# Single-head attention and ternary ffn in one loop, with the reads of the mixture's sums spread over it

## The chip, the core and the metric

The kernel runs on one core of a Trainium2 chip. Its engines work side by side, each through its own queue in order: PE (TensorE; its weight loads are shown as PEld), DVE (VectorE), ACT (ScalarE), POOL (GpSimd) and SP (SyncE, which here only issues DMAs). They wait for one another through semaphores. The metric is the device time of one execution in microseconds (us); lower is better.

## The reference, cut to what matters

A decoder of four layers works on x of 128 sequences x 64 positions x 128 features, with a context of the same shape. Each layer has an attention, a cross attention and an ffn; after each step comes `x = layernorm(x + step(x))`. The change touches the three steps of layer 0:

```python
# step 1, "attn": a mixture of 8 experts, two of them for each token
probs = softmax(x @ gate_w + gate_b); topw, topi = top_k(probs, 2); topw /= topw.sum()
out_e = gelu_tanh(x @ w1[e] + b1[e]) @ w2[e] + b2[e]
y = sum over the two chosen e of topw * out_e
# step 2, "xattn": one head of width 128
q, k, v = x @ Wq + bq, ctx @ Wk + bk, ctx @ Wv + bv
y = softmax(q @ k.T / sqrt(128)) @ v
# step 3, "ffn": ternary weights
W = clip(round(W / scale), -1, 1), scale = max(mean(|W|), 1e-8)     # for W1 and W2
y = gelu(x @ W1.T + b1) @ W2.T + b2
```

Everything is fp32.

## The kernel before, in words

The 8192 tokens stay in SBUF as 16 chunks `X[0..15]` of 512 tokens (four tiles of 128 tokens x 128 features). The twelve steps run one after the other (`steps`, L1890); each runs over the chunks. A tile framework gives out buffers, sets the semaphores, and places the instructions of each engine in a fixed order by its own estimate of when each could run; inside the mixture's loop the order is written out (`issue_after`).

**The mixture** (`Sorted`, L472; driven by `moe_top2`, L912). The tokens of a batch are sorted by expert into groups of 256 rows. Batches are chunks 0 to 4 and 5 to 15. `all_groups` (L848) runs over the groups of both batches: SP loads the expert's weights (L730), POOL gathers the rows from DRAM by indirect DMA (L747), PE transposes them (L758), hidden layer (L772, L774) and output (L785, L786) follow, and SP writes the rows to a DRAM buffer `l_rout` (L787). Beside it run generators (`aside`): the plan of the next batch, and `finish` (L794) of the batch before. `finish` takes a step for each token tile: two indirect reads on POOL (L805), and three steps later on DVE the weighted sum (L815, L817) and statistics (L818); when a chunk's four tiles are summed, `end` (L820) makes its LayerNorm on DVE (L827 to L357, a reciprocal square root in several small instructions) and ACT applies it (L378). A cost list and a length (`total - 4` groups) say when each generator takes its next step. The first batch's sums lie in the loop of the second batch's groups. The second batch's sums are a generator of its own, `moe_end` (L897).

**The single-head attention** (`xattn_single`, L949) is a software pipeline over turns i = -3 to 15 with five steps a turn (L1036): `scores` of chunk i+1 (L999, then maximum, Exp and sum), `turned_weights` of i (transposes, L1014), `projections` of i+2 (q, k by `projected`, L937; v with its bias as a matmul of bf16 rows that `bv` holds, L981), `values` of i (L1026, L1032, LayerNorm applied on ACT) and `sources` of i+3. `sources` calls `moe_done` (L917): it steps `moe_end` four times, and further until the chunk is summed; then it transposes the context (L930) and x (L325).

**The ternary ffn** (`ffn_ternary`, L1042) first makes the ternary weights on ACT, DVE and PE (L1049 to L1063), then goes through the chunks with `hidden` of c ahead of `output` of c-1 (`pipelined`, L406). `hidden` transposes x (L325), adds the output bias to x on POOL (`with_bias`, L393) and makes four hidden blocks with Gelu (L1072, L1074). `output` (L1082) makes 16 products of 128 x 128, each matmul instruction recorded twice; DVE adds x (L399) and takes the statistics (L366, L368), and POOL applies the LayerNorm (`ln_apply`, L380).

The differential attention `attn_diff` follows. It uses two buffers `VX` (L1095), which POOL fills with zeros and two columns of a mask (L1114, L1116) before use.

PSUM has eight banks: `bank` (L315) takes from three of them, `wide` (L318) from five.

Of the kernel before, what the change touches and what calls it, by code (L numbers as in the profile page):

```python
# [22 lines left out]
P = 128  # L23
# [211 lines left out]
def tile_decoder(ctx: ExitStack, tc: tile.TileContext, a, out):  # L235
# [69 lines left out]
    def row(n):  # L305
        return rows[:, _ROW_AT[n][0] : _ROW_AT[n][1]]
# [64 lines left out]

    def ln_apply(c, r, mv, y, store=False, on_act=False):
        if on_act:
            s = sm.tile([P, TPC], F32, tag="lns", name="lns")
            V.scalar_tensor_tensor(s, mv[:, :, 0], -1.0, y, ALU.mult, ALU.mult)
        for t in range(TPC):
            if on_act:
                A.activation(X[c][:, t, :], r[:, t, :], AF.Identity, bias=s[:, t : t + 1], scale=y[:, t : t + 1])  # L378
            else:
                G.tensor_scalar(X[c][:, t, :], r[:, t, :], mv[:, t, 0:1], y[:, t : t + 1], ALU.subtract, ALU.mult)  # L380
        if store:
            nc.sync.dma_start(out=out_v[c], in_=X[c])

    def layernorm(c, r, store=False, on_act=False):

        v = sm.tile([P, TPC], F32, tag="lnv", name="lnv")
        mv = ln_stats(r, v)
        ln_apply(c, r, mv, rsqrt(v, TPC, "ln"), store, on_act)

# [82 lines left out]
    class Sorted:  # L472
# [4 lines left out]
        def __init__(s, which, top, batches, src, wg, bias, act, cap=None, store=False, scattered=None):  # L477
            s.which, s.top, s.batches, s.src, s.wg, s.bias, s.act, s.cap, s.store = which, top, batches, src, wg, bias, act, cap, store
            s.at, s.loaded, s.done, s.carry = {}, {}, set(), None
            s.row_tiles, s.turned, s.between = {}, {}, None  # L480
# [367 lines left out]
        def all_groups(s):  # L848
# [10 lines left out]
            for b in range(nb):  # L859
# [5 lines left out]
                if b > 0:  # L865
                    aside.append([s.finish(b - 1), [1] * s.finish_steps(b - 1), 0, 2, total - 4])
                for g in range(total):
# [23 lines left out]
                for x in aside:  # L891
                    assert x[2] == len(x[1]) and next(x[0], None) is None
            s.output(*last)


    moe = Sorted("l0", 2, MOE_BATCHES, [a["x"]], "gatew", "gateb", AF.Gelu_apprx_tanh)
    moe_end = moe.finish(len(MOE_BATCHES) - 1)  # L897

# [18 lines left out]
    def moe_done(c):  # L917

        for _ in range(TPC):
            next(moe_end, None)  # L920
        while c not in moe.done:
            next(moe_end)
# [25 lines left out]

    def xattn_single():  # L949
# [3 lines left out]
        st = {}  # L953

        rest = work("tmp", (P, D), "bvrest")
        V.tensor_copy(rest, row("l0xbv"))
        bv = work("tab", (P, 2, P), "bvparts", BF16)
        part = work("tmp", (P, D), "bvpart", BF16)
        V.memset(bv[:, 0, :], 1.0)
        for k in range(3):  # L960
            V.tensor_copy(part, rest)
            if k == 0:
                V.tensor_scalar(bv[:, 1, :], part, ident[:, 0:1], None, ALU.mult)
            else:
                V.scalar_tensor_tensor(bv[:, 1, :], part, ident[:, k : k + 1], bv[:, 1, :], ALU.mult, ALU.add)
            if k < 2:
                V.tensor_tensor(rest, rest, part, ALU.subtract)
        ring = work("e", (P, 4, TPC, D), "v1")
# [6 lines left out]
        def projections(c):  # L975
            s = st[c]
            s["q"] = projected(w[:, 0, :], s["xT"], "qT", col("l0xbq"))
            s["k"] = projected(w[:, 1, :], CTX[c], "kT", col("l0xbk"))

            v = bank("v1_ps")  # L980
            mm(v.rearrange("p (n d) -> p n d", n=4), bv[:32, 0, :], bv[:32, 1, None, :].to_broadcast([32, 4, D]), start=True, stop=False, skip_group_check=True)  # L981
            for f in range(2):
# [52 lines left out]

        for i in range(-3, NC):  # L1036
            for step, c in ((scores, i + 1), (turned_weights, i), (projections, i + 2), (values, i), (sources, i + 3)):
                if 0 <= c < NC:
                    step(c)


    def ffn_ternary():  # L1042
        w = W[2]
        wt = work("tab", (P, 2, FK, P), "tern")
        for n in range(2):
            src = w[:, 4 * n : 4 * n + 4, :].rearrange("p k m -> p (k m)")
            t = work("tmp", (P, 512), "absw")
# [39 lines left out]

# [6 lines left out]
    V.tensor_copy(identh, ident)  # L1094
    VX = [const.tile([P, BPC * 8 * 34], F32, tag=f"vx{n}", name=f"vx{n}") for n in range(2)]  # L1095

# [786 lines left out]
    def ffn_switch():  # L1883
# [32 lines left out]
```

## Time and profile before

| | us |
|---|---|
| runs shown: median (lowest to highest) | 3282.17 (3279.47 to 3289.09) |
| the profiled execution, its own time | 3278.03 |
| its span, first to last instruction | 3276.3 |
| mean granted TensorE clock | 0.946 |

Busy time over the span, and of the groups that the change touches:

| row | count | busy us | mean ns | idle before, and what ended it |
|---|---|---|---|---|
| PE, whole span | 47184 | 2882.3 (88%) | | |
| DVE, whole span | 7074 | 1973.2 (60%) | | |
| ACT, whole span | 3106 | 1614.1 (49%) | | |
| POOL, whole span | 1548 | 1521.4 (46%) | | |
| L805 POOL indirect read got<-l_rout | 192 | 194.4 | 1012 | 148.7, most by issue |
| L747 POOL indirect gather aux<-x | 156 | 159.9 | 1025 | 56.9, most by issue |
| L380 POOL x<-xb (all steps) | 304 | 238.6 | 797 | 267.5, by DVE ln_y L345 |
| L772 PE h_ps<-ebT,rw (both mixtures) | 992 | 241.2 | 387 | 8.6, most by DMA rw |

The counts of L805 and L380 include later steps; of L805, 40 lie between 207.5 and 347.8 us (first batch) and 88 between 411.9 and 526.7 us (second batch).

How to read the rows of the profile: a group's row gives line, engine, operation, the tile written and the tiles read with their shape, the count, busy time and mean. A row of waits says which engine and line waited for which engine and line: us in total, times, the longest. A row of the timeline gives start, duration and instruction, "x4" for four merged ones, and in brackets how long the engine idled before and what ended that. A row of stages gives for each engine the busy time in that window and, in brackets, the number of instructions. Matmuls overlap, so the cost of one is read from the distance between starts.

### The profile page before, as it was taken

What the parts mean: (1) busy time and instruction counts of PE and PEld (TensorE: products, weight loads), DVE (VectorE), ACT (ScalarE), POOL (GpSimd) and SP (SyncE); (2) the same over time, 40 slices, a digit from 0 to 9 for tenths busy, and PEclk for the clock granted to TensorE, in tenths of its full rate; (3) what the DMA queues carried; (4) which work ended last, traced back from release to release, by engine and by line L of the source; (5) the groups of instructions that cost most, each with busy time, mean ns of one, the idle gap of its engine ahead of it and who ended that gap; (6) DMA issues with size and microseconds to landing.
All of it is one profiled execution on the core that took longest, in us unless ns stands there. A gap on an engine that the chain in (4) does not pass through costs nothing. (4 is left out here: it accounts for less than half of the span.)

```text
span 3276.3 us, 110323 instructions
## 1 busy us (share of the span) xinstructions
PE 2882.3 (88%) x47184; PEld 2115.1 (65%) x47184; DVE 1973.2 (60%) x7074; ACT 1614.1 (49%) x3106; POOL 1521.4 (46%) x1548
## 2 busy tenths in 40 slices
PE   5999967999987999999999989998888569998993
PEld 3888834666665777766677767774444336776793
DVE  3733267557777666433256656666778886666246
ACT  3544457445543565333355545643444555654553
POOL 4477473454555344311234445556566322446154
PEclk9999988999998999999999989989988789998997
DMA  5578710000002000000000000000000000001684
GB/s 142 160 214 248 220 52 28 8 1 3 3 3 76 19 4 4 6 1 1 5 11 4 4 5 4 4 13 1 1 1 2 9 1 16 18 15 46 181 266 147
DMA packets 142459, 159.23 MB, mean 49 GB/s; under 512 B 16720, under 2 KB 118096, under 8 KB 141968
## 3 DMA queue, kind: packets, MB, share of 16 engines
q1 hardware_dynamic: 128064, 123.65, 12.7%
q0 software_dynamic: 13184, 27.03, 3.2%
q8 instruction: 370, 6.06, 0.7%
q10 hardware_dynamic: 720, 1.50, 0.1%
q14 instruction: 121, 0.99, 0.1%
HBM read 121.44 MB, written 30.67 MB: 46 GB/s over the span
## 5 line engine op out<-in xcount | busy, mean ns | idle before, releaser
L1183 DVE TENSOR_REDUCE m<-s_ps 128x8 f32<-128x512 f32 x640 | 397.5, 683 | 144.4 <-PE s_ps L1411 50.8
L1232 ACT ACTIVATE e<-t_ps 128x512 f32<-128x512 f32 x640 | 330.0, 601 | 150.7 <-PE t_ps L1225 150.2
L380 POOL TENSOR_SCALAR x<-xb,lnmv,ln_y 128x128 f32<-128x128 f32 x304 | 238.6, 797 | 267.5 <-DVE ln_y L345 267.5
L1250 PE MATMUL av_ps<-vx,e 128*64 128x18 f32 (+1 forms) x10240 | 341.3, 216 | 5.6 <-issue 5.3
L1250 PEld LDWEIGHTS av_ps<-vx,e 128*64 128x64 f32 x10240 | 322.9, 140 | 25.9 <-issue 18.7
L1127 POOL TENSOR_SCALAR eb<-qT,small 128x512 f32<-128x512 f32 x80 | 131.2, 1640 | 431.5 <-ACT qT L943 200.9
L774 ACT ACTIVATE hT<-h_ps,aux 128x256 f32<-128x256 f32 x496 | 206.6, 470 | 208.4 <-PE h_ps L772 102.3
L1213 PE MATMUL t_ps<-eb,kT 32*64 32x128 f32 x10240 | 281.3, 285 | 4.4 <-DVE m L1183 2.2
L805 POOL DMA_INDIRECT got<-l_rout,pli x192 | 194.4, 1012 | 148.7 <-issue 57.7
L772 PE MATMUL h_ps<-ebT,rw 128*128 128x256 f32 x992 | 241.2, 387 | 8.6 <-DMA rw<-in_l0w_dram 4.5
L785 PEld LDWEIGHTS yg<-rw,hT 128*128 128x128 f32 x1984 | 241.8, 192 | 6.4
L1213 PEld LDWEIGHTS t_ps<-eb,kT 32*64 32x64 f32 x10240 | 198.1, 132 | 71.1 <-DVE m L1183 25.6
L785 PE MATMUL yg<-rw,hT 128*128 128x128 f32 x1984 | 242.1, 276 | 0.0
L1175 PE MATMUL s_ps<-eb,qT 32*64 32x256 f32 x5120 | 217.5, 399 | 20.8 <-POOL eb L1127 9.8
L786 DVE TENSOR_TENSOR yo<-yg,aux 128x256 f32<-128x256 f32 x124 | 52.6, 424 | 267.5 <-PE yg L785 264.4
L1255 DVE RECIPROCAL rc<-av_ps 128x32 f32<-128x32 f32 (+1 forms) x192 | 61.7, 321 | 240.7 <-PE av_ps L1250 240.3
L772 PEld LDWEIGHTS h_ps<-ebT,rw 128*128 128x128 f32 x992 | 182.8, 194 | 31.1 <-DVE ebT L760 6.3
L747 POOL DMA_INDIRECT aux<-in_x_dram,plt x156 | 159.9, 1025 | 56.9 <-issue 26.8
L1125 ACT ACTIVATE eb<-qT,small 128x512 f32<-128x512 f32 x160 | 106.8, 715 | 129.3 <-POOL qT L1352 124.1
L380 POOL TENSOR_SCALAR x<-r,lnmv,ln_y 128x128 f32<-128x128 f32 x68 | 54.4, 813 | 225.0 <-DVE ln_y L345 225.0
L1127 POOL TENSOR_SCALAR eb<-kT,small 128x512 f32<-128x512 f32 x80 | 145.9, 1823 | 22.1 <-ACT kT L945 11.3
L1175 PEld LDWEIGHTS s_ps<-eb,qT 32*64 32x64 f32 x5120 | 114.3, 134 | 60.2 <-issue 15.2
(429 smaller groups left out, 6414.5 us busy)
## 6 DMA issues: line engine op xcount, KB each, us to landing
rw<-in_l0w_dram SPq DMA_DIRECT2D x78, 512.0 KB
rw<-in_l3w_dram SPq DMA_DIRECT2D x46, 512.0 KB
l_rout<-yo SPq DMA_DIRECT2D x124, 128.0 KB
aux<-xd SPq DMA_DIRECT2D x46, 128.0 KB
aux<-in_l0b_dram SPq DMA_DIRECT2D x78, 66.0 KB
xd<-vx SPq DMA_DIRECT2D x5, 1024.0 KB
x<-in_x_dram SPq DMA_DIRECT2D x16, 256.0 KB
cin<-in_ctx_dram SPq DMA_DIRECT2D x16, 256.0 KB
```

The lines of the kernel that those rows point to most:

```text
L380: G.tensor_scalar(X[c][:, t, :], r[:, t, :], mv[:, t, 0:1], y[:, t : t + 1], ALU.subtract, ALU.mult)
L747: s.gather = G.indirect_dma_start(out=eb[:, i, :], out_offset=None, in_=x[:, :], in_offset=bass.IndirectOffsetOnAxis(ap=tokens[:, 2 * g + ...
L772: s.pe = mm(ps[:, j * GR : (j + 1) * GR], w1[:, (k + j) * P : (k + j + 1) * P], ebT, start=True, stop=True)
L774: s.act_ins = A.activation(hT[k + j], ps[:, j * GR : (j + 1) * GR], s.act, bias=v[:, k + j : k + j + 1])
L785: s.pe = mm(y[:, i * P : (i + 1) * P], hT[k][:, i * P : (i + 1) * P], w2[:, k, :], start=(k == 0), stop=(k == FK - 1))
L805: s.gather = G.indirect_dma_start(out=got[i][k][:, t, :], out_offset=None, in_=s.rout[b][:, :], in_offset=bass.IndirectOffsetOnAxis(ap=whe ...
L1127: ins = (G if h == 2 else V).tensor_scalar(dst, x, mine, None, ALU.mult)
L1175: mm(ps[g][j * S : (j + 1) * S, u * 256 : (u + 1) * 256].rearrange("p (h k) -> p h k", h=4), rows32(s["q"], g)[:, b], rows32(s["eb"], g)[: ...
L1183: last = V.tensor_reduce(s["m"][:, g, 2 * hf : 2 * hf + 2, :].rearrange("p t h -> p (t h)"), ps[g].rearrange("p (n k) -> p n k", k=S), AX. ...
L1213: mm(ps[g][i * S : (i + 1) * S].rearrange("p (a u j q) -> p a u j q", u=2, a=2, j=2)[:, :, u, j, :], rows32(s["k"], g)[:, b], rows32(s["eb ...
L1232: last = A.activation(e[:, g, :], ps[g], AF.Exp, scale=scale)
L1250: mm(av[j * S : (j + 1) * S, 8 * (u - u0) + n, :], ev[:, n // 2, n % 2, u, j, :], vx[:, 2 * (2 * hf + u) + j, n, :], start=True, stop=True,)
```

## The change

- Attention and ffn run in one loop of turns i = -3 to 17. The ffn is two chunks behind: in turn i `turned`, `hidden` and `output` work on chunk i-2, `hidden` and `output` of a chunk in the same turn. The ternary weights are made after turns -3 and -2.
- `summed`, a single step of the mixture's sums, stands in four places of a turn. `moe_done` only steps further while the chunk isn't summed.
- The first batch's sums get twice the length (`stretch = 2`), so that some half of their steps are left when the group loop ends; `moe_sums` takes those first and then the second batch's.
- The ffn's output bias is no longer added to x on POOL; it opens the output's accumulation as a matmul of bf16 rows (`bias_rows`), as the attention's value bias did. Both sets of rows, and the hidden blocks, lie in the `VX` buffers, which are defined earlier.
- `ln_apply` can run on DVE; the ffn does so for chunks 0 to 7 and stays on POOL for 8 to 15.
- q and k of the attention take their PSUM from `wide` and no longer from `bank`.

```diff
@@ ln_apply
-                G.tensor_scalar(X[c][:, t, :], r[:, t, :], mv[:, t, 0:1], y[:, t : t + 1], ALU.subtract, ALU.mult)
+                (V if on_dve else G).tensor_scalar(X[c][:, t, :], r[:, t, :], mv[:, t, 0:1], y[:, t : t + 1], ALU.subtract, ALU.mult)
@@ Sorted.all_groups
-                    aside.append([s.finish(b - 1), [1] * s.finish_steps(b - 1), 0, 2, total - 4])
+                    s.rest = s.finish(b - 1)
+                    aside.append([s.rest, [1] * s.finish_steps(b - 1), 0, 2, s.stretch * (total - 4)])
@@
-    moe_end = moe.finish(len(MOE_BATCHES) - 1)
+    moe.stretch = 2
+
+    def moe_sums():
+        yield from moe.rest
+        yield from moe.finish(len(MOE_BATCHES) - 1)
+
+    moe_end = moe_sums()
@@ moe_done
-        for _ in range(TPC):
-            next(moe_end, None)
         while c not in moe.done:
             next(moe_end)
@@
-    def projected(w, srcT, name, bias=None):
+    def projected(w, srcT, name, bias=None, bank=bank):
...
+    VX = [const.tile([P, BPC * 8 * 34], F32, tag=f"vx{n}", name=f"vx{n}") for n in range(2)]
+
+    def bias_rows(bias, place, name):
+
+        both = VX[place][:, 2048:2176].bitcast(BF16).rearrange("p (z d) -> p z d", z=2)
+        rest, part = work("tmp", (P, D), f"{name}rest"), work("tmp", (P, D), f"{name}part", BF16)
+        V.tensor_copy(rest, bias)
+        V.memset(both[:, 0, :], 1.0)
+        for k in range(3):
+            V.tensor_copy(part, rest)
+            if k == 0:
+                V.tensor_scalar(both[:, 1, :], part, ident[:, 0:1], None, ALU.mult)
+            else:
+                V.scalar_tensor_tensor(both[:, 1, :], part, ident[:, k : k + 1], both[:, 1, :], ALU.mult, ALU.add)
+            if k < 2:
+                V.tensor_tensor(rest, rest, part, ALU.subtract)
+        return both[:32, 0, :], both[:32, 1, None, :].to_broadcast([32, 4, D])
@@ xattn_single, projections
-            s["q"] = projected(w[:, 0, :], s["xT"], "qT", col("l0xbq"))
-            s["k"] = projected(w[:, 1, :], CTX[c], "kT", col("l0xbk"))
+            s["q"] = projected(w[:, 0, :], s["xT"], "qT", col("l0xbq"), wide)
+            s["k"] = projected(w[:, 1, :], CTX[c], "kT", col("l0xbk"), wide)
@@
-        for i in range(-3, NC):
-            for step, c in ((scores, i + 1), (turned_weights, i), (projections, i + 2), (values, i), (sources, i + 3)):
-                if 0 <= c < NC:
-                    step(c)
-
-
-    def ffn_ternary():
-        w = W[2]
+        b2 = bias_rows(row("l0fb2"), 1, "b2t")
+        tern = W[2]
         wt = work("tab", (P, 2, FK, P), "tern")
-        for n in range(2):
-            src = w[:, 4 * n : 4 * n + 4, :].rearrange("p k m -> p (k m)")
+
+        def ternary(n):
+            src = tern[:, 4 * n : 4 * n + 4, :].rearrange("p k m -> p (k m)")
...
+        def summed(_):
+            next(moe_end, None)
+
+        def turned(c):
+            st[c] = {"xT": transposed(X[c], "xT")}
+
         def hidden(c):
-            xT = transposed(X[c], "xT")
-            xb = with_bias(c, "l0fb2")
-            hT = work("h", (P, FK, 512), "hT")
+            hT = st[c]["h"] = VX[c % 2][:, : FK * 512].rearrange("p (k t) -> p k t", k=FK)
             for k in range(0, FK, 2):
                 ps = [wide("h_ps") for _ in range(2)]
                 for j in range(2):
-                    mm(ps[j], wt[:, 0, k + j, :], xT, start=True, stop=True)
+                    mm(ps[j], wt[:, 0, k + j, :], st[c]["xT"], start=True, stop=True)
                 for j in range(2):
                     A.activation(hT[:, k + j, :], ps[j], AF.Gelu, bias=col("l0fb1")[:, k + j : k + j + 1])
-            return hT, xb
-
-        def output(c, state):
-            hT, xb = state
+
+        def output(c):
+            hT = st.pop(c)["h"]
             y = bank("y")
+            mm(y.rearrange("p (n d) -> p n d", n=4), *b2, start=True, stop=False, skip_group_check=True)
             for t in range(TPC):
                 for k in range(FK):
-                    mm(y[:, t * P : (t + 1) * P], hT[:, k, t * P : (t + 1) * P], wt[:, 1, k, :], start=(k == 0), stop=(k == FK - 1))
-            add_norm(c, y, xb)
-
-        pipelined(range(NC), hidden, output)
+                    mm(y[:, t * P : (t + 1) * P], hT[:, k, t * P : (t + 1) * P], wt[:, 1, k, :], start=False, stop=(k == FK - 1), skip_group_check=True)
+
+            layernorm(c, added(c, y), on_dve=c < 8)
+
+
+        for i in range(-3, NC + 2):
+            for step, c in (
+                (scores, i + 1), (summed, i), (turned, i - 2), (turned_weights, i), (projections, i + 2), (summed, i), (hidden, i - 2),
+                (summed, i), (values, i), (sources, i + 3), (output, i - 2), (summed, i),
+            ):
+                if step == summed or 0 <= c < NC:
+                    step(c)
+            if i in (-3, -2):
+                ternary(i + 3)
@@ steps
-        moe_top2, xattn_single, ffn_ternary, attn_diff, xattn_causal, ffn_routed,
+        moe_top2, xattn_single, None, attn_diff, xattn_causal, ffn_routed,
...
+        if step is None:
+            continue
```

More of the change, by code (lines that the diff above doesn't have):

```diff
@@ L370, in ln_stats, with ln_apply @@
         return mv
-    def ln_apply(c, r, mv, y, store=False, on_act=False):
+    def ln_apply(c, r, mv, y, store=False, on_act=False, on_dve=False):
         if on_act:
@@ L379, in ln_apply, with layernorm @@
             else:
-                G.tensor_scalar(X[c][:, t, :], r[:, t, :], mv[:, t, 0:1], y[:, t : t + 1], ALU.subtract, ALU.mult)
+                (V if on_dve else G).tensor_scalar(X[c][:, t, :], r[:, t, :], mv[:, t, 0:1], y[:, t : t + 1], ALU.subtract, ALU.mult)
         if store:
             nc.sync.dma_start(out=out_v[c], in_=X[c])
-    def layernorm(c, r, store=False, on_act=False):
+    def layernorm(c, r, store=False, on_act=False, on_dve=False):
         v = sm.tile([P, TPC], F32, tag="lnv", name="lnv")
         mv = ln_stats(r, v)
-        ln_apply(c, r, mv, rsqrt(v, TPC, "ln"), store, on_act)
+        ln_apply(c, r, mv, rsqrt(v, TPC, "ln"), store, on_act, on_dve)
     def with_bias(c, name):
@@ L479, in __init__ @@
             s.at, s.loaded, s.done, s.carry = {}, {}, set(), None
-            s.row_tiles, s.turned, s.between = {}, {}, None
+            s.row_tiles, s.turned, s.between, s.stretch, s.rest = {}, {}, None, 1, None
             s.rout = [dram.tile([s.count(b) * GR, D], F32, tag=f"{which}_rout{b}", name=f"{which}_rout{b}") for b in range(len(batches))]
@@ L891, in all_groups @@
                 for x in aside:
-                    assert x[2] == len(x[1]) and next(x[0], None) is None
+                    assert x[0] is s.rest and s.stretch > 1 or x[2] == len(x[1]) and next(x[0], None) is None
             s.output(*last)
     moe = Sorted("l0", 2, MOE_BATCHES, [a["x"]], "gatew", "gateb", AF.Gelu_apprx_tanh)
-    moe_end = moe.finish(len(MOE_BATCHES) - 1)
+    moe.stretch = 2
[3 more added lines that the diff above has]
+    moe_end = moe_sums()
     CIN = []
@@ L953, in xattn_single @@
         st = {}
[L955 to L967, printed above, removed]
+        bv = bias_rows(row("l0xbv"), 0, "bv1")
         ring = work("e", (P, 4, TPC, D), "v1")
@@ L976, in projections @@
             s = st[c]
-            s["q"] = projected(w[:, 0, :], s["xT"], "qT", col("l0xbq"))
-            s["k"] = projected(w[:, 1, :], CTX[c], "kT", col("l0xbk"))
+            s["q"] = projected(w[:, 0, :], s["xT"], "qT", col("l0xbq"), wide)
+            s["k"] = projected(w[:, 1, :], CTX[c], "kT", col("l0xbk"), wide)
             v = bank("v1_ps")
-            mm(v.rearrange("p (n d) -> p n d", n=4), bv[:32, 0, :], bv[:32, 1, None, :].to_broadcast([32, 4, D]), start=True, stop=False, skip_group_check=True)
+            mm(v.rearrange("p (n d) -> p n d", n=4), *bv, start=True, stop=False, skip_group_check=True)
             for f in range(2):
@@ L1094, in tile_decoder @@
     V.tensor_copy(identh, ident)
-    VX = [const.tile([P, BPC * 8 * 34], F32, tag=f"vx{n}", name=f"vx{n}") for n in range(2)]
     def rows32(t, g):
```

## The prediction

> **What bounds the kernel now.** The edited stretch is the top-2 mixture, the single-head attention and the ternary ffn. The table of stages comes first; columns: window, its length, then busy us (instructions) of PE, PEld, DVE, ACT and POOL, granted TensorE clock, DMA share, GB/s.
>
> ```profile
> 54.00:408.30 354.30, 328.98 (x2195) 293.90 (x2194) 142.62 (x426) 164.75 (x380) 217.74 (x214) 0.99 0.70 200
> 408.30:443.00 34.70, 21.30 (x169) 13.40 (x169) 13.48 (x65) 15.27 (x32) 24.08 (x24) 0.80 0.21 58
> 443.00:453.00 10.00, 4.51 (x60) 2.87 (x58) 10.00 (x75) 5.62 (x12) 7.67 (x8) 0.98 0.16 48
> 453.00:527.00 74.00, 55.12 (x441) 29.92 (x441) 56.87 (x396) 49.66 (x130) 56.83 (x57) 0.79 0.18 51
> 527.00:571.00 44.00, 33.94 (x348) 20.49 (x349) 35.61 (x222) 35.09 (x91) 4.60 (x4) 0.93 0.03 10
> 571.00:578.00 7.00, 1.83 (x9) 1.43 (x8) 6.94 (x39) 3.15 (x7) 0.00 (x0) 0.50 0.00 1
> 578.00:700.00 122.00, 121.68 (x697) 89.52 (x698) 58.96 (x321) 54.37 (x83) 60.43 (x69) 0.98 0.02 5
> ```
>
> The ffn (578 to 700) is bound by PE at full clock: 122 of 122 us. The attention (408.3 to 571) is not: PE is part busy at a clock of 0.79. From 571 to 578 PE stands almost still while DVE makes the ternary weights. What the attention waits for is read from the waits, then the POOL rows:
>
> ```profile
> POOL got L805 <- DMA l_rout<-yo: 34.4, 1, 34.4
> DVE r L815 <- DMA got<-l_rout,pli: 23.2, 19, 6.9
> DVE r L817 <- DMA got<-l_rout,pli: 14.5, 22, 1.0
> ```
>
> POOL idles 34.4 us, until the last mixture rows land at 411.9, and then issues 88 indirect reads at 1.31 us each (411.91, 413.21, 414.52, ...) until 527.7. DVE waits for them. A chunk costs eight reads, 10.5 us of POOL; so the attention turns run at about 10.6 us while PE needs far less. Two rows side by side give PE's need: between reads, an attention chunk runs from the transposes at 545.00 to those at 551.01, 6.0 us; an ffn chunk repeats every 7.55 us (L399 at 643.86 and 651.41).
>
> **The change, part by part.** Times of 408.3 and after are of before.
>
> *One loop.* PE work of a full turn is 6.0 + 7.55 + 0.31 for the new bias matmul (L981 to L986, 417.21 to 417.52) = 13.9 us. The other engines in a turn:
> - POOL: 8 reads x 1.31 = 10.5; from chunk 8 on 4 x 0.79 of L380 besides, when the reads are nearly over. No longer the bound: it has 13.9 us or more where it had to do with 10.6.
> - DVE: 56.87 busy us over seven turns (453 to 527) = 8.1, plus 58.96/16 = 3.7 of the ffn, plus the new normalization (below) = 12.6.
> - ACT, by start-to-start spacing where back to back: four copies x 0.5, p1T 0.3, q and k 1.2, four Exp 0.85, two LayerNorm applications x 1.55 (470.22 to 471.77), four Gelu x 0.59 (4.74 for 8): 9.8. New: Exp and Gelu alternate. The built program has 26 table loads in the loop where before has 2 (L1005, L1074), about two a turn.
>
> The price of a switch is the place where a rule speaks against this change. The trace shows switches both ways in the conv stage:
>
> ```profile
> 2304.29 1.28 ACT L1727 ACT_TABLE_LOAD   x1
> 2305.59 0.68 ACT L1727 ACTIVATE g<-dn_ps,cols 64x512 f32<-64x512 f32 x1
> 2306.29 1.28 ACT L1680 ACT_TABLE_LOAD   x1
> 2307.58 0.60 ACT L1680 ACTIVATE units<-ye_ps 128x512 f32<-128x512 f32 x1
> ```
>
> Each load takes 1.28 and the next activation starts at once: 1.29 a switch, 2.6 a turn, ACT 12.4. The Trainium skill, "ScalarE: Activation LUTs", section "What ACT_TABLE_LOAD costs", puts a drain of about 1.38 us on top, 2.66 in all, and its section on table sets says to batch activations by set, which one loop undoes. By the rule ACT would need 15.2 and exceed PE. I take the row and keep the rule as a rival.
>
> Which wait ends last in a turn: the output matmuls follow the hidden ones in the same turn and need the fourth Gelu. Ahead of it ACT has xT 0.5, p1T 0.3, q, k 1.2, Exp 0.85, v 0.5, one application 1.55, two loads 2.6, four Gelu 2.4 = 9.9, starting 0.75 after the turn does (transposes 0.53 and a handoff estimated at 0.2): 10.7. PE is at the output after 9.5 (0.53 + 0.35 + 0.96 + 0.96 + 0.31 + 1.03 + hidden 3.5 + values 0.6 + context and x transposes 1.0 + bias 0.31) and stalls about 1.2; the remaining output (3.7 less two matmuls, 0.5) and the scores (0.65) end the turn near 14.7. For stalls shared by three engines at 90% I add 0.8: **15.5 us a turn**, between 13.9 (none) and 18.
>
> Turns -3 to 1 have no ffn. Before needs 35 us for them (408.3 to 443); I keep that: the ternary's DVE work (about 7 us, 571 to 578) comes in, the 8.5 us that ACT waited behind L378 for chunk 5's reads shrinks. Turns 2 to 12 are full: 11 x 15.5 = 170. Turns 13 to 17 lose transposes (1.0), projections (3.3), scores and values one after another: PE 12.9 + 9.6 + 8.9 + 7.9 + 7.9 = 47, with 5 of stalls 52. Sum 257, against 408.3 to 700 = 291.7: **-35**. Inside it are the gap of 7 us (571 to 578) and the low clock.
>
> *First batch's reads.* About 10 of 40 reads leave the mixture's loop for its tail, the rest spread out. There POOL was back to back (130.67 busy in 205 to 380, issue gaps besides) and PE waited 7.2 us for row gathers queued behind the reads. Now POOL needs per group two gathers and 0.6 reads, 3.4 us against 3.6 for a group. I take **-5**: 0 if the weight loads (DMA share 0.84 there, and 4.5 us of PE waits for rw) become the limit, -8 at best. The moved 10 reads fill the 34.4 us in which POOL idled; without that cover they would put 13 us before batch two's reads, which chunk 5 does not need until turn 2's end.
>
> *Bias as matmul.* Removes 16 x 1.29 of POOL (L393), counted at nothing since POOL wasn't the bound; adds 16 x 0.31 on PE, counted above.
>
> *LayerNorm applied on DVE for chunks 0 to 7.* Keeps them from queueing behind up to 88 reads on POOL. Not in the trace on this shape; the nearest rows are 0.40 for a 128x512 single-source op (L1060, so 0.1 to 0.2 for a quarter) and 0.27 spacing for the two-source L1032. I take 0.2, 0.8 a chunk, in DVE's 12.6; at 0.27 it is 1.1, still under PE.
>
> *q and k in the five-buffer PSUM pool.* New waits: the third hidden matmul needs Exp's bank, the second half of the values the first Gelu's. By the queue sums above both come within 0.3 us of ready; they belong to the 0.8. Behind a late one stand the whole PE queue and thus the turn; up to 1 us a turn if ACT is late.
>
> *Bias rows, Abs* now run in the mixture's plan (DVE 12.8 to 17.9 busy of each 20 us, ACT about 11; Abs 2 x 0.64): hidden; uncovered, about 5 us once.
>
> *VX memsets* (1.94 + 0.48, twice) leave the start of the program (0.9 and 7.3 us) for POOL's queue between ffn and the next attention. The second starts when the last output is read, at PE's ffn end, and ends 2.5 us later; POOL's next work started 4.9 us after that end (704.88 to 700.0). Nothing; uncovered, 2.5.
>
> **Sum.** -35 - 5 = -40. The profiled execution took 3278.0 (span 3276.3), giving 3238 for it; the median shown is 4.1 higher, so **3242**.
>
> **Rivals.**
> 1. *The switch costs the rule's 2.66.* The fourth Gelu comes 2.7 later and PE can hide little: a turn of 17.6, 11 x 2.1 + two late turns x 2 = +27: **3269**. For: Exp and Gelu alternate as in no other stage. Against: the rows above. 15%.
> 2. *The coupling eats the overlap: slower.* In-order ACT holds hidden's Gelus behind applications that wait for DVE, and DVE's own queue waits for values and output. If attention and ffn run one after the other, a turn is 10.6 + 7.55 + 2.6 = 20.8: 11 x 5.3 = +58, **3300**. It decides from 15.5 + 40/11 = 19.1 a turn. For: ACT waited 8.5 us behind one such application (435.16). Against: in the loop's order Exp has almost a turn before it is used, and the reads have slack. 10%.
> 3. *PE-bound without stalls*, as the ffn was: 13.9 a turn, tail 48: 11 x 1.6 + 4 = -22, **3220**. 12%.
> 4. *Reads still pace it* or early turns lengthen by 20 us or more: within the noise of 3272 to 3292. 3%.
> The forecast has 60%.
>
> **Numbers.** 0.3% is 9.8 us, about what a measurement tells from no change. Faster: forecast, rival 3, nearly all of rival 1 = 0.85; same 0.04; slower 0.11. Range: down to rival 3 less 4 (a better mixture), up past rival 1: 3216 to 3275; outside stand rival 2 and the ends of the others.
>
> **What would show it.** In the changed profile: turns of 15 to 16 us in the loop (spacing of the output's L399); a granted clock near 1.0 there; 26 table loads in it of 1.28 with an activation right behind; POOL's reads no longer waited for by DVE after turn 2; PE's wait for row gathers in the mixture below 3 us; the last ffn output near 657. Wrong would be: a turn over 17 with PE waiting for Gelu (rival 1, or ACT's order), DVE over 95% busy in the loop, or reads that still set the pace.

## The result, and the profile after

| | before | after |
|---|---|---|
| runs shown: median (lowest to highest), us | 3284.21 (3279.47 to 3289.09) | 3240.35 (3239.41 to 3250.23) |
| ratio of after to before, 95% interval | | 0.987 (0.985 to 0.990) |
| the profiled execution, us | 3278.03 | 3240.21 |
| its granted TensorE clock | 0.946 | 0.952 |
| end of the mixture on PE | 408.6 | 409.1 |
| end of the last ffn output on PE | 700.2 | 652.1 |
| from the one to the other | 291.55 | 243.04 |

The gain lies behind the mixture, in the merged loop: 48.5 us there, none in the mixture. Between the medians it is 43.9 us; between the two profiled executions 37.8. The rest of the program, which the change leaves alone (ACT runs through it in the same order of instructions, PE nearly so), took 2576.1 us after the last ffn output in the profile of before and 2586.3 in that of after. A second profile of the changed kernel has 2586.5. The profiled execution of before lies 6.2 us below the median of before, so more than half of the ten may be scatter between executions. Laid side by side from the last ffn output on, the PE records of before and of the two profiles after keep within about 1 us for the first 1000 us; the difference comes later, and not at the same places in the two. So the next attention does not start later than before, and the ten are not taken apart further.

The table of stages of the changed kernel, with its own bounds (columns: window, its length, busy us and instructions of PE, PEld, DVE, ACT and POOL, granted clock, DMA share, GB/s):

```profile
54.00:408.90 354.90, 330.37 (x2196) 295.37 (x2196) 138.78 (x402) 161.73 (x371) 216.55 (x214) 0.99 0.70 200
408.90:440.00 31.10, 25.50 (x233) 15.69 (x231) 24.82 (x141) 22.05 (x52) 21.15 (x21) 1.00 0.24 69
440.00:587.00 147.00, 146.94 (x1078) 97.95 (x1078) 127.71 (x806) 126.33 (x255) 70.18 (x72) 1.00 0.11 32
587.00:652.00 65.00, 63.67 (x427) 43.05 (x427) 42.12 (x236) 42.19 (x82) 20.79 (x27) 1.00 0.03 9
```

The third row is the one to look at. In the full turns PE is busy for 146.9 of 147 us at a granted clock of 1.00, where the attention before had 0.79. DVE is at 87% and ACT at 86%, POOL at 48%. In this window PE (its matmul row) waits for no other engine at all.

One full turn on PE, from the transposes of the ffn's x (L325) to those of the next turn (timeline; columns: start, duration, then the instruction; PE's matmuls are recorded twice, so that "x8" of the values are four instructions):

```profile
468.77 0.66 PE L325 MATMUL xT_ps<-ident,x 128*128 128x128 f32 x4
...
472.64 3.70 PE L1081 MATMUL h_ps<-xT,tern 128*128 128x512 f32 x8
476.27 0.65 PE L1036 MATMUL y<-v,p1T 64*64 64x128 f32 x8
476.85 0.66 PE L935 MATMUL ctx_ps<-ident,cin 128*128 128x128 f32 x4
477.35 0.60 PE L325 MATMUL xT_ps<-ident,x 128*128 128x128 f32 x4
477.88 0.65 PE L1036 MATMUL y<-v,p1T 64*64 64x128 f32 x8
...
479.64 0.56 PE L1009 MATMUL s_ps<-kT,qT 128*64 128x64 f32 x10
480.13 3.17 PE L1091 MATMUL y<-tern,vx 128*128 128x128 f32 x26
483.23 0.45 PE L1009 MATMUL s_ps<-kT,qT 128*64 128x64 f32 x6
483.61 0.65 PE L325 MATMUL xT_ps<-ident,x 128*128 128x128 f32 x4
```

It takes 14.84 us, and nothing in it has idle time in brackets. The values (L1036) come in two pieces, the first output bank ahead of the transposes and the second behind them, and each piece takes 0.58 us (start to start). Before, all 16 records together took 0.60:

```profile
549.92 0.67 PE L1026 MATMUL y<-v,p1T 64*64 64x128 f32 x16
550.52 0.66 PE L930 MATMUL ctx_ps<-ident,cin 128*128 128x128 f32 x4
```

In the program each bank takes its products from one half of the rows. In one piece the built order alternates between the banks, and with them between the halves; here eight records in a row use one half. That this is why the pieces are slower was not tested apart from the order. The scores (L1009), in two pieces, take 0.49 and 0.38 where one piece took 0.62. That is 0.56 + 0.25 = 0.81 us that the work itself doesn't need; in every third turn the scores are in one piece, and it is 0.56.

In the mixture PE no longer waits for row gathers. The waits of PE in 200 to 409 us, first before, then after:

```profile
PE ebT_ps L758 <- DMA aux<-in_x_dram,plt: 7.2, 9, 1.5
PE h_ps L772 <- DMA rw<-in_l0w_dram: 4.5, 3, 2.6
```

```profile
PE h_ps L772 <- DVE ebT L760: 8.9, 3, 6.6
PE h_ps L772 <- DMA rw<-in_l0w_dram: 1.0, 1, 1.0
PE h_ps L772 <- DVE yo L786: 0.3, 1, 0.3
```

Before it had 7.2 us for gathers and 4.5 for rw, 11.7 in all; now 10.2, and 8.9 of them for a copy on DVE. The timeline of DVE at the first of these stalls tells why:

```profile
335.70 0.41 DVE L760 COPY ebT<-ebT_ps 128x256 f32<-128x256 f32 x1
342.61 0.35 DVE L815 SCALAR_TENSOR_TENSOR r<-got,plw,x 128x128 f32<-128x128 f32 x1 [6.50 <-DMA got<-l_rout,pli]
342.88 0.42 DVE L786 TENSOR_TENSOR yo<-yg,aux 128x256 f32<-128x256 f32 x1
343.21 0.42 DVE L760 COPY ebT<-ebT_ps 128x256 f32<-128x256 f32 x1
```

A weighted sum (L815) of the first batch stands in DVE's queue ahead of what the current group needs (L786, L760). It waits until 342.6 for a read that POOL issues only at 339.62 and 340.92, and L786 and L760 wait behind it. The same happens at 367 to 374 us. With the sums stretched over twice the groups, reads come later (ten of the 40 behind the last row gather), and the order in which the framework set DVE's instructions has two sums too early. By the reads that they wait for, these two are among the steps that are left when the group loop ends. Only the steps taken inside that loop are held in place by `issue_after`; the rest are stepped in the attention's turns, and the framework was free to move them up. A kernel that holds them back was not run.

### The profile page after: what moved, and what is told of

It reads as the page before. It is cut to its first block, busy times and chain, and to the rows that moved or that the text cites. A ratio compares the mean times of both kernels' runs of the same rounds, so it can differ in the third digit from the quotient of the medians.

```text
span 3238.4 us, 110324 instructions
## 1 busy us (share of the span) xinstructions
PE 2889.3 (89%) x47200; PEld 2120.7 (65%) x47200; DVE 1979.3 (61%) x7116; ACT 1638.5 (51%) x3130; POOL 1470.8 (45%) x1500
## 5 line engine op out<-in xcount | busy, mean ns | idle before, releaser
L380 POOL TENSOR_SCALAR x<-xb,lnmv,ln_y 128x128 f32<-128x128 f32 x240 | 188.7, 798 | 173.6 <-DVE ln_y L345 173.6
L785 PEld LDWEIGHTS yg<-rw,hT 128*128 128x128 f32 x1984 | 241.5, 192 | 6.4
L785 PE MATMUL yg<-rw,hT 128*128 128x128 f32 x1984 | 241.9, 275 | 0.0
L380 POOL TENSOR_SCALAR x<-r,lnmv,ln_y 128x128 f32<-128x128 f32 x100 | 79.4, 807 | 293.3 <-DVE ln_y L345 246.9
L786 DVE TENSOR_TENSOR yo<-yg,aux 128x256 f32<-128x256 f32 x124 | 52.5, 424 | 260.8 <-PE yg L785 260.7
```

Of the source, the lines that this page charges most:

```text
L380: (V if on_dve else G).tensor_scalar(X[c][:, t, :], r[:, t, :], mv[:, t, 0:1], y[:, t : t + 1], ALU.subtract, ALU.mult)
L785: s.pe = mm(y[:, i * P : (i + 1) * P], hT[k][:, i * P : (i + 1) * P], w2[:, k, :], start=(k == 0), stop=(k == FK - 1))
```

## The experiments

Twelve runs followed. They and the first result fell on chips of two kinds. On one (the first result, and the last four runs) before takes 3284 and 3288 us; on the other (the first eight runs) it takes 3518 and 3524. Each kernel is judged against before on its own chip. The first kind is called A here, the second B. B turned out to be limited by something else in this stretch (below), so what was asked of A could not all be answered on B.

| kernel | chip | median us | ratio to before (95%) | mixture ends | from there to the last ffn output |
|---|---|---|---|---|---|
| changed | A, first result | 3240.35 | 0.987 (0.985 to 0.990) | 409.1 | 243.0 |
| two_loops | B | 3469.57 | 0.986 (0.984 to 0.987) | 465.6 | 338.2 |
| gelu_id | B | 3443.19 | 0.978 (0.976 to 0.979) | 466.7 | 301.3 |
| stretch1 | B | 3500.89 | 0.993 (0.991 to 0.996) | 502.1 | 324.1 |
| values_last | B | 3451.70 | 0.981 (0.979 to 0.983) | 461.9 | 307.3 |
| after_2 (changed) | B | 3433.86 | 0.975 (0.972 to 0.977) | 460.0 | 301.8 |
| two_loops_2 | B | 3472.17 | 0.986 (0.983 to 0.989) | 460.9 | 337.8 |
| stretch1_2 | B | 3498.86 | 0.993 (0.990 to 0.995) | 503.4 | 321.0 |
| values_last_2 | B | 3445.73 | 0.978 (0.976 to 0.981) | 464.1 | 311.4 |
| after_3 (changed) | A | 3243.52 | 0.987 (0.985 to 0.988) | 414.6 | 245.0 |
| turn_order | A | 3271.17 | 0.995 (0.993 to 0.996) | 407.2 | 272.6 |
| turn_order_bias | A | 3273.19 | 0.995 (0.994 to 0.997) | 406.2 | 272.7 |
| pool_norm | A | 3255.53 | 0.990 (0.989 to 0.992) | 409.2 | 245.2 |

**Is it the merge?** `two_loops` keeps every edit but runs the attention's turns first and the ffn after them:

```diff
-        for i in range(-3, NC + 2):
+        for i in range(-3, NC):
             for step, c in (
-                (scores, i + 1), (summed, i), (turned, i - 2), (turned_weights, i), (projections, i + 2), (summed, i), (hidden, i - 2),
-                (summed, i), (values, i), (sources, i + 3), (output, i - 2), (summed, i),
+                (scores, i + 1), (summed, i), (turned_weights, i), (projections, i + 2), (summed, i),
+                (summed, i), (values, i), (sources, i + 3), (summed, i),
             ):
...
+        for i in range(NC + 1):
+            if i < NC:
+                turned(i)
+                hidden(i)
+            if i > 0:
+                output(i - 1)
```

> All edits of the change stay except the merge: the attention's turns -3 to 15 run first, with the reads of the sums in the same four places, and the ternary ffn follows in a loop of its own, a chunk's output behind the next chunk's hidden. Theory (the merge carries the gain, because PE's 13.9 to 14.8 us of a turn fill the time in which the attention waits for 10.6 us of reads): attention and ffn are one after the other again, 408 to about 565 and 122 + 5 (16 bias matmuls of 0.31) for the ffn: the last ffn output near 692 to 700, time 3270 to 3285, ratio to before 0.997 to 1.002. Rival (the spread reads and the early ternary weights carry it): within 10 us of the changed kernel, 3240 to 3250, ratio near 0.988.

> As for two_loops, now beside the changed kernel. Theory (the merge carries the gain, the longer stretch for the first batch's sums carries nothing where the mixture is bound by PE): on a chip like the first, the last ffn output near 692 to 700, 40 to 48 us behind the changed kernel. On a chip like the second the mixture's part is separate: its end some 36 us before that of stretch1, as was seen, and the merge worth the rest, 30 us. Rival: the spread of the sums carries all on every chip, and this kernel comes within 10 us of the changed one.

On B it is 38 us slower than the changed kernel beside it (3472.2 against 3433.9), and the stretch behind the mixture is 36 us longer (337.8 against 301.8). So the merge is worth 36 us there. But two_loops is still 51 us faster than before on that chip (3472.2 against 3523.7), so there the merge is not all: neither theory holds as it was put, since on B a second part pays, the longer stretch (next). On A two_loops was not run; the 48.5 us of A were not split by experiment. That the merge carries them there is read from the trace alone, and the spread of the reads may have a share.

**The first batch's reads.** `stretch1` puts all of them back into the mixture's loop:

```diff
-    moe.stretch = 2
+    moe.stretch = 1
```

> The first batch's sums are all made in the mixture's loop again (stretch 1 for 2). The prediction's step (PE waits for row gathers behind reads, 5 us gained by moving ten reads out): the mixture ends some 5 us later than in the changed kernel, 3243 to 3246. Theory now (the gather waits were exchanged for two waits of 6.5 and 7.4 us in which DVE, in order, stands before a weighted sum whose read has not landed, while the transposed rows of a group wait behind it): no net difference in the mixture, its end at 407 to 410, PE's waits for gathers back at 6 to 8 us and those for the copy of the rows gone; total within 4 us of 3240.

> As for stretch1. On a chip like the first: mixture's end within 3 us of the changed kernel's, PE's waits for gathers back at 6 to 8 us, the two long waits of DVE gone, total within 5 us. Rival: on every chip the ten reads cost the mixture what they cost on the second, some 36 us. If the chip is like the second, 30 to 40 us more than the changed kernel.

On B it is 65 us slower than the changed kernel beside it (3498.9 against 3433.9), where 30 to 40 were expected. The mixture ends 43 us later (503.4 against 460.0), and the stretch behind it is 19 us longer (321.0 against 301.8). They lie ahead of turn 2, the first full one: 77 us from the mixture's end to there, against 57. PE stands there 21.3 us in one piece for an Exp and 14.8 for a copy of x (stretch1_2, waits of PE in 503 to 592):

```profile
PE p_ps L1024 <- ACT e L1015: 21.3, 1, 21.3
PE qT_ps L945 <- ACT xT L332: 14.8, 1, 14.8
```

So on B the longer stretch pays more than the merge. The two parts do not simply add: taken away one at a time they cost 65 and 38 us, and the whole change brings 90 (3523.7 to 3433.9). On A stretch1 was not run. The five profiles with stretch 2 end the mixture there at 406.2 to 414.6, 409.3 on average, against 408.6 in the one of before: no gain in the mixture, within this scatter. What the edit does for the early turns on A was not measured.

**The table loads.** `gelu_id` has Identity where the ffn has Gelu:

```diff
-                    A.activation(hT[:, k + j, :], ps[j], AF.Gelu, bias=col("l0fb1")[:, k + j : k + j + 1])
+                    A.activation(hT[:, k + j, :], ps[j], AF.Identity, bias=col("l0fb1")[:, k + j : k + j + 1])
```

> The ffn's Gelu is left out: Identity in its place, which shares its table with Exp, so that the 26 table loads of the loop go and nothing else changes. Theory (the loop is bound by PE, whose matmuls stand back to back for 14.8 us a turn): 0 to 5 us less than the changed kernel's 3240, from the early turns and the last four. Rival (ACT's chain up to the fourth Gelu sets the turn, a switch at the trace's 1.29 us): two switches a turn go, 11 x 1 to 2.6 = 11 to 28 us less, 3212 to 3229. Second rival (a switch costs 2.66 with its drain): up to 50 us less.

Of the loop's 26 loads one, at its start, is left, and the stretch behind the mixture takes 301.3 us against 301.8 in after_2 (another chip of kind B). On B they cost nothing that can be seen; its turns of 16 to 21 us show other waits. For A the price is read from the trace of the changed kernel (ACT's timeline):

```profile
475.42 1.28 ACT L1083 ACT_TABLE_LOAD   x1
476.71 2.42 ACT L1083 ACTIVATE vx<-h_ps,cols 128x512 f32<-128x512 f32 x4
```

All 26 loads of the loop take 1.283 us, and here the activation begins 1.29 us after the load did. The 2.66 us of the Trainium skill's page ("ScalarE: Activation LUTs", "What ACT_TABLE_LOAD costs") is not seen here. Whether 1.29 costs anything on PE was not tried on A.

**The order of a turn.** The split values were the part that looked like a flaw. `values_last` moves the values behind the transposes of the next sources:

```diff
-                (summed, i), (values, i), (sources, i + 3), (output, i - 2), (summed, i),
+                (summed, i), (sources, i + 3), (values, i), (output, i - 2), (summed, i),
```

> In a turn the attention's values follow the transposes of the next chunk's sources instead of standing ahead of them; the built order then has the 16 value matmuls alternate between the two output banks (and the two halves of the rows), where in the changed kernel eight for one bank are followed by eight for the other, and has the score matmuls in one piece. Theory (PE is the bound, and the turn of 14.8 us instead of 13.9 comes from values taking 1.18 us instead of 0.60, scores 0.88 instead of 0.62): 0.6 to 0.85 us less a turn, 11 to 12 turns: 6 to 10 us less than the changed kernel, 3230 to 3234, the spacing of the output's addition 13.9 to 14.1. Rival (a turn's length is set by the chain through ACT and DVE, the PE records only fill it): spacing stays near 14.7, time within 3 us of 3240, and PE shows idle time or longer records elsewhere.

> The changed kernel itself, as the measure for its companions on the same chip. On the chip of the first result its ratio to before was 0.987 and its turns took 14.7 us. On the chip of the four runs before this one, where before takes 3518 us, waits for the issue of instructions and slower reads make turns of 17 to 21 us: there it should stand at 0.981 to 0.984, a few us behind values_last, with its mixture ending near 464; on a chip like the first, at 0.986 to 0.989.

> As for values_last. On a chip like the first, where PE stands back to back: 0.6 to 0.85 us less a turn, spacing of the output's addition 13.9 to 14.1, 6 to 10 us less than the changed kernel beside it. Rival (PE's records only fill a turn that another engine sets): spacing stays near 14.7 and the time within 3 us. On a chip like the second, where turns of 17 us and more are not set by PE: no difference over 5 us by either.

It is slower than the changed kernel beside it, 3445.7 against 3433.9 us, where no difference over 5 us was expected (the intervals of the two ratios still touch). Yet one of its turns without a stall shows the size of the piece (values_last_2, timeline of PE):

```profile
692.99 0.60 PE L325 MATMUL xT_ps<-ident,x 128*128 128x128 f32 x4
...
701.30 0.67 PE L1036 MATMUL y<-v,p1T 64*64 64x128 f32 x16
701.90 0.39 PE L1088 MATMUL y<-vx 32*128 32x512 bf16 x1
702.22 3.84 PE L1091 MATMUL y<-tern,vx 128*128 128x128 f32 x32
705.99 0.69 PE L1009 MATMUL s_ps<-kT,qT 128*64 128x64 f32 x16
706.60 0.66 PE L325 MATMUL xT_ps<-ident,x 128*128 128x128 f32 x4
```

Values in one piece are 0.60 us, scores 0.61, and the turn is 13.61. The turns between such ones had the values bank by bank again and took longer, so the next kernel held the order on PE in every turn (`turn_order`): each value matmul behind the one before it, the first behind the transposes, and the scores behind the last output product.

```diff
+                        with tc.issue_after(st["last"].ins) if "last" in st else nullcontext():
+                            st["last"] = mm(
...
+                    with tc.issue_after(st["output"].ins) if "output" in st else nullcontext():
+                        mm(ps[j * S : (j + 1) * S, p, :], s["q"][:, b], s["k"][:, b], start=True, stop=True)
```

> The changed kernel again, beside its three companions. On a chip like the first 0.985 to 0.990 of before, turns of 14.5 to 14.9 us on PE without a wait; on a chip like the second 0.972 to 0.978, turns of 17 to 21 us while the reads run and 14.5 to 15 after them.

> As values_last, but with the order of a turn held on PE in every turn (values_last had it in every other turn alone; in the turns between, its value matmuls stood bank by bank among the transposes and waited for DVE): transposes of the sources, then the 16 value matmuls alternating between the two banks, then the output, then the 16 score matmuls in one piece. Theory (PE is the bound and the order makes 14.8 us of the 13.9 that its work takes): a full turn that no wait lengthens measures 13.5 to 13.9 on PE from transposes to transposes, values 0.6 and scores 0.62; on a chip like the first 8 to 11 us less than the changed kernel beside it, on a chip like the second 0 to 10 us less, since stalls of another kind set most turns there. Rival (the turn is set elsewhere and PE would wait): PE shows waits for Gelu or for DVE of 0.5 us and more a turn, and the time stays within 4 us.

On A it loses 27.7 us to the changed kernel beside it (3271.2 against 3243.5; the intervals of the two ratios are far apart), and a turn takes 17.2 us. The theory fell: in the program as it was built, PE cannot keep up the shorter order. Its timeline:

```profile
518.43 0.43 PE L1040 MATMUL y<-v,p1T 64*64 64x128 f32 x2
520.17 0.66 PE L1040 MATMUL y<-v,p1T 64*64 64x128 f32 x14 [1.31 <-ACT vx L1087]
520.76 5.44 PE L1095 MATMUL y<-tern,vx 128*128 128x128 f32 x32
526.13 0.69 PE L1012 MATMUL s_ps<-kT,qT 128*64 128x64 f32 x16
```

The second bank of the values is one that a hidden block held. It comes free when the first Gelu has read it, and in this order PE stands 1.31 us for that Gelu. Then a second loss comes: the output takes 5.37 us (520.76 to 526.13) where it took 3.77 in the turn above. The table of short windows shows what changed (the clock is the third figure from the end):

```profile
518.00:520.00 2.00, 0.86 (x5) 0.45 (x4) 1.33 (x9) 1.97 (x3) 1.42 (x2) 1.00 0.16 45
520.00:522.00 2.00, 1.83 (x20) 1.66 (x21) 1.13 (x5) 2.00 (x5) 1.67 (x2) 0.68 0.24 59
522.00:524.00 2.00, 2.00 (x11) 2.00 (x11) 1.86 (x12) 0.81 (x2) 1.39 (x3) 0.50 0.14 39
524.00:526.00 2.00, 2.00 (x19) 2.00 (x18) 0.98 (x7) 0.00 (x0) 0.93 (x1) 0.97 0.24 66
```

After the stall PE's granted clock is 0.68, then 0.50, and nearly full (0.97) some 4 us later. In the changed kernel the first piece of the values needs only the bank that is already free; the transposes follow, and by the time the second piece starts the Gelu is done. Its 0.56 to 0.81 us a turn of slower matmuls are the price of never standing still.

But the run changed more than PE's order. With it the framework also set ACT's queue anew, and ACT's timeline of this turn shows what that did:

```profile
510.33 0.58 ACT L334 COPY xT<-xT_ps 128x512 f32<-128x512 f32 x1 [4.71 <-PE xT_ps L325]
...
516.44 1.68 ACT L380 ACTIVATE x<-r,lns,fln 128x128 f32<-128x128 f32 x4
518.13 1.28 ACT L1087 ACT_TABLE_LOAD   x1
519.43 2.42 ACT L1087 ACTIVATE vx<-h_ps,cols 128x512 f32<-128x512 f32 x4
```

ACT idles 4.7 us until the turn's first transposes, and then all eight LayerNorm applications of the turn (L380) stand ahead of the Gelus. The first Gelu starts 9.85 us into the turn; in turns 3 to 12 of the changed kernel, where ACT takes some of this work ahead of the transposes, it starts after 7.0 to 8.4. With such an ACT order the stall might not be there. So turn_order shows that its own built order is worse than the changed kernel's; whether PE's shorter order would pay with ACT's queue held as it was is not shown.

**Bias back on POOL.** `turn_order_bias` takes the ffn's bias matmul off PE again:

```diff
-            mm(y.rearrange("p (n d) -> p n d", n=4), *b2, start=True, stop=False, skip_group_check=True)
...
-            layernorm(c, added(c, y), on_dve=c < 8)
+            layernorm(c, added(c, y, xb), on_dve=c < 8)
```

> turn_order with the ffn's output bias added to x on POOL again (16 x 1.29 us) in place of the bias matmul (16 x 0.31 us on PE). Theory (PE is the bound, POOL has 10.5 us of reads in a turn of nearly 14 and so some room): 11 to 16 turns shorter by 0.31, another 3 to 5 us less. Rival (POOL's queue: the addition stands among the reads, 10.5 + 1.3 = 11.8 us a turn and the reads come later; the buffer of the sum lives longer): no gain or up to 10 us more, with DVE waiting for reads or for xb.

No difference to turn_order (3273.2 against 3271.2), and the stretch behind the mixture is the same 272.7. PE waits for the Gelu in each turn here too (14.3 us over 11 turns), so 0.31 us of PE work less can't shorten it. On top of the changed kernel's own order it was not tried.

**LayerNorm on POOL.** `pool_norm` undoes one edit:

```diff
-            layernorm(c, added(c, y), on_dve=c < 8)
+            layernorm(c, added(c, y), on_dve=False)
```

> The ffn's LayerNorm is applied on POOL for all chunks, as before the change (POOL 4 x 0.79 us a chunk), in place of DVE for chunks 0 to 7 (4 x 0.27). Theory (it keeps the applications from standing behind the reads; nothing in the loop reads an ffn's result before the next attention, so PE does not wait for it): POOL gets 10.5 + 3.2 = 13.7 us a turn, close to the turn, and the reads end later; on a chip like the first within 5 us of the changed kernel. Rival (POOL becomes the bound, or the buffers of the sums come free late): 10 to 25 us more, turns above 15 with DVE waiting for reads.

By its runs it is 12 us slower than the changed kernel (ratio 0.990, 0.989 to 0.992, against 0.987, 0.985 to 0.988), which is more than the theory had and at the low end of the rival. Its profile doesn't show where: that execution took 3246.06 us, 9.5 below its median, and the stretch behind the mixture is 245.2 us as in after_3, with POOL at 97 us busy of 147 instead of 73. So the edit pays, but the place of the 12 us stays open.

On A no kernel here beats the changed one.

## Why the prediction was right, and where it wasn't

The total was right: 3242 forecast, 3240.4 measured. The direction and the place of the gain were argued and came true; that the total is met within 2 us is luck. It holds errors that partly cancel: the loop brought 48.5 us and not 35, the mixture none and not 5, and 10 us of the profiled gain are missing in stages that no step spoke of.

*The loop, part by part* (turns counted by the start of L1024 on PE, from the changed kernel's first profile):

| | forecast | measured | |
|---|---|---|---|
| turns -3 to 1 | 35 | 31.2 | mixture's end to 440.25 |
| turns 2 to 12 | 11 x 15.5 = 170 | 11 x 14.7 = 161.8 | 440.25 to 602.02 |
| turns 13 to 17 | 52 | 50.1 | to 652.1 |
| sum | 257 | 243.0 | |

- *PE needs 13.9 us a turn*: right for matmuls in one piece. The undisturbed turn of values_last_2 took 13.61 (on B).
- *The sum of queues, 14.7, with a stall of 1.2 us for the fourth Gelu*: right in its length (14.7 on average), wrong in what fills it, so the agreement is luck. PE has no such stall. The Gelus end 10.4 us into the turn shown (479.13), near the forecast's 10.7, but PE comes to the output later than forecast, and the first products and some scores cover the rest. What makes the turn longer than 13.9 is work: the values and scores in pieces, 0.56 to 0.81 us. The stall of 1.31 us in turn_order is another one, for the first Gelu.
- *Plus 0.8 for stalls shared by three engines*: the term that was mis-sized. There were none: PE's matmul row has no wait in the window. It is 8 to 9 of the 14 us by which the loop beat the forecast. An allowance for stalls was added to a sum that already held one.
- *Early turns keep their 35*: 4 us too many. The ternary weights fitted in and the granted clock was 1.00 instead of 0.80. The tail was 2 us shorter than forecast.
- *A table switch costs the row's 1.29*: the row held, the loads are 1.283 us with the activation right behind. In the changed kernel PE never waits for ACT in the full turns, so the loads cost it no wait there; no run on A left them out. The turn of 17.6 that the first rival forecast with the page's 2.66 did not come.
- *Reads off the path*: right. In 440 to 587 us DVE has no wait for a read, and POOL's reads now wait for DVE (33.3 us for L827), which costs nothing.
- *The mixture's -5*: wrong. PE's waits for gathers went, as the step said, but the step had no entry for DVE's queue: two sums stand there before their reads have landed, and the copies for the next group behind them. What was gained came back as a new wait (11.7 us of PE waits before, 10.2 after). On B the same edit is worth 65 us, 43 of them in the mixture, of which the step says nothing.
- *q and k in the five-buffer pool*: named as part of the 0.8; the second half of the values did need the first Gelu's bank, as written, and this is the wait that the split hides. q and k were not moved back by themselves.
- *LayerNorm applied on DVE, 0.2 us each*: 0.27 was measured (474.60, four in 1.10 us), the step's own upper figure; DVE stayed at 87%.
- *VX memsets hidden*: right. The second starts at 652.25 us and ends at 654.2, its copies at 654.7; POOL's next work starts at 656.55.
- *The rivals*: the serial coupling did not come, and the reads do not set the pace. The third rival (PE-bound without stalls) has the mechanism that the trace shows, PE busy for 146.9 of 147 us with no wait; only its 13.9 us a turn was too short, since it did not have the split matmuls. Its total of 3220 also counted on the mixture's 5 us.

## What to carry to other kernels

When a sum over queues already contains the last wait of a turn, don't add an allowance for stalls on top; look for work that the built order can put into the wait instead. An order that looks wasteful on PE may be what keeps it from standing: before straightening it, find which buffer the delayed half waits for, price a stall with the lower clock that may follow it, and see what the new order does to the other queues. A step that is moved later in a loop also moves in every in-order queue that consumes it: here the reads left POOL's way and the sums came into DVE's.

## What the hardware showed besides

*A stall of 1.3 us can cost more than itself.* In turn_order nine of the ten full turns with a wait of 1.31 us have 3.4 us at a granted clock of 0.50 beside it (520.73 to 524.14 in the turn shown); the 16 output products take 1.6 us more, and the turn is 17.16 us (509.58 to 526.74) where 13.61 were measured without either. In the tenth such turn (wait at 621.82) the clock is 1.00 from 621 to 626: its output takes 4.24 us and the turn 16.05. In the changed kernel's early turns PE stood 1.32 and 1.44 us at a stretch (before 428.56 and 437.08), with the clock at 1.00. So the length of the wait alone does not decide it, and what does is not shown. The Trainium skill ("TensorE: Matmul & The Clock Gate", "Part 1: The HAM clock gate") has the clock fall after an idle window of about 3.4 us; here it fell at 1.31 us of standing.

*The same program waits elsewhere on another chip.* On the chips of kind B the rows of PE in the mixture look like this for some 14 us (after_2, timeline of PE, a few of its rows, then the stretch as a whole):

```profile
251.65 0.37 PE L785 MATMUL yg<-rw,hT 128*128 128x128 f32 x1 [1.03 <-issue]
252.35 0.37 PE L785 MATMUL yg<-rw,hT 128*128 128x128 f32 x1 [0.33 <-issue]
253.75 0.37 PE L785 MATMUL yg<-rw,hT 128*128 128x128 f32 x1 [1.03 <-issue]
```

```profile
244.00:258.00 14.00, 4.89 (x14) 3.32 (x13) 0.00 (x0) 0.84 (x2) 9.19 (x10) 0.51 0.19 48
```

The matmuls of L785 come one at a time with "issue" ahead of them, a wait that no record explains; on A 16 records take 1.95 us. All that time POOL issues gathers and reads one behind the other, and the DMA engines are only 19% busy. While the reads run in the loop of B, PE's rows show such waits too (8.5 us ahead of L1091 and 3.0 ahead of L1009 in 540 to 660) and turns take 16 to 21 us; after the last read (661.7) 1.4 us of them are left up to 720, and the next full turns take 16.5 and 14.9 us. What stretch 2 changes in the mixture on such a chip is where the reads lie: all 40 are still issued before its end, but ten of them behind the last row gather, which goes out at 413.9 us in after_2 and at 461.3 in stretch1_2. What holds the issue up was not found.
